# Exact first-layer outputs kept in their PSUM bank, and one ring of five banks, in an AdaLN block with a mixture of experts

## The chip, the cores and the metric

The kernel runs on one core of a Trainium2 chip. A core has five engines, each with its own in-order queue: TensorE (PE) for matmuls, VectorE (DVE) and ScalarE (ACT) for elementwise work, GpSimd (POOL) for elementwise work and indirect transfers, and SyncE (SP), which here only issues transfers. Matmul results land in PSUM, a memory of eight banks of 512 float32 columns by 128 partitions; everything else is in SBUF. The metric is the device time of one execution in microseconds (us). A smaller time is better.

## The reference

The reference is one transformer block on `x` of shape 2 x 2048 x 256: a layer norm with modulation, windowed attention with 16 heads, a residual add, a second layer norm with modulation, and a mixture of 8 experts of which each token uses 2. Only the expert part matters here. In short:

```python
logits = x @ gate_w.T + gate_b
probs = softmax(logits); topk_prob, topk_idx = top_k(probs, 2)
for c in range(2):
    # each token goes to a slot of its expert, up to 640 slots per expert and choice
    xb = slots of expert e
    hmid = relu(xb @ W1[e] + b1[e])        # 256 -> 1024
    yb = hmid @ W2[e] + b2[e]              # 1024 -> 256
    y = y + yb[slot of token] * prob
```

All of it is float32. The kernel keeps the precision by splitting every matmul operand into an upper part, rounded to a shorter float format, and a lower part, which is the exact value minus the upper one. A product is then three matmuls: upper with upper, upper with lower, lower with upper.

## The kernel before

The first 700 us or so are attention; the experts follow, and the first expert's first work is woven into the end of attention. The experts' work is cut into items: item `q` is an expert `e` with a range of row tiles of 128 slots (the list `items`). For experts 2 to 6 the first item has six tiles and is called wide here, and further items of two tiles, called short here, follow under an `If` on the number of filled slots (`further`, L1314 marks its branches). The items 0, 1 and 5 have two tiles and are placed by hand; from item 2 on a scheduler arranges the instructions of each stretch between two branches.

An item has eight steps `f`, one for each 128 of the 1024 hidden columns.
- `first_layer(q, f)` multiplies the turned slots `xT` with W1 into a PSUM bank `ph`. A wide item's 768 columns don't fit one bank, so it takes two chunks of 384 with a bank each. Six matmuls fill a chunk (L230, in `passes`). Then L1008 on ScalarE writes `hh`, the upper part of the relu, L1009 on VectorE computes the exact relu into an SBUF tile `r`, and L1010 on VectorE writes the lower part `hl = r - hh`. L1010 runs once for the whole step, over up to 768 columns. Both `hh` and `hl` carry the name `hm` in the profile.
- `second_layer(q, f)`, two steps later (`LAG`), multiplies `hm` with W2 and accumulates into `y`, three matmuls for each row tile.
- `scale_of` makes the tile `gw` of gates: L1044 on ScalarE and L1047 on VectorE, whose inputs `gbr` and `gw` both lie in SBUF. It runs in one step for each row tile of the item.
- `turn_slots` transposes the slots of a later item through a bank `tp_x` (L966) and splits them with L131 on ScalarE and L135 on VectorE.
- At the end of an item `results` adds the bias (L1063, VectorE, `ys<-y,b`), and `give` multiplies by the gates (L1073, GpSimd, `ys<-ys,gw`) and adds the rows to the output with indirect transfers (L1074, GpSimd). They run on GpSimd while TensorE is already in the next item.

PSUM during the experts: `ph` has three banks of its own, `y` three, and a ring of two serves everything else, the turned slots among it. `r` has one buffer, `hm` three for each part. In item 0 the ring of attention, six banks, serves all.

The lines of the scheduler's hints (`keep_in_program_order`) are not touched.

Of the kernel before, what the change touches and what calls it, by code (L numbers as in the profile page):

```python
# [8 lines left out]
FP = mybir.dt.float32  # L9
# [3 lines left out]
ALU = mybir.AluOpType  # L13
# [4 lines left out]
P = 128  # L18
# [10 lines left out]
def adaln_block_kernel(  # L29
# [18 lines left out]
    nc = tc.nc  # L48
# [4 lines left out]
    E, _, FF = w1.shape  # L53
# [35 lines left out]
    ring = {}  # L89

    def bank(name, shape=(P, 512)):
        return ring["pool"].tile(list(shape), FP, tag="ring", name=name, bufs=ring["bufs"])
# [132 lines left out]
    def passes(out_, pairs, start=True, stop=True, **kw):  # L225

        last = len(pairs) - 1
        for n, ((ah, al), (bh, bl)) in enumerate(pairs):
            for i, (a, b) in enumerate(((ah, bh), (ah, bl), (al, bh))):
                nc.tensor.matmul(  # L230
                    out=out_, lhsT=a, rhs=b,
                    start=start and n == 0 and i == 0,
                    stop=stop and n == last and i == 2, **kw,
                )
# [694 lines left out]
    def load_slots(q, more=0):  # L929

        e, tiles = items[q]
        hi = items[q + more][1].stop
        m = hi - tiles.start
        if q < 2:
            xt = (cl if q else early).tile([P, m, ROW], FP, tag="xt", name=f"xt_{q}", bufs=1)
        else:
            w = WIDE if m > 4 or not more else 4
            xt = mp.tile([P, w, ROW], FP, tag=f"xt{w}", name=f"xt_{q}", bufs=1 if w == 4 else 2)
        r0 = (E - e) * BUF - hi * P
        nc.sync.dma_start(  # L940
            out=xt[:, 0:m, :], in_=xbuf[r0 : r0 + m * P, :].rearrange("(n p) d -> p n d", p=P)
        )
        for i in range(q, q + more + 1):
            t = items[i][1]
            xts[i] = xt[:, hi - t.stop : hi - t.start, :]
# [28 lines left out]
    def first_layer(q, f):  # L974
        e, tiles = items[q]
        wa = experts[e].parts()[0]
        xh, xl = xTs[q]
        bias = b1T[:, e * NF + f : e * NF + f + 1]
        W = len(tiles) * P
        pool, w, bufs = (mp, WIDE * P, 1) if q else (early, W, 1)  # L980
        per = w // W
        if f % per == 0:
            first_layer.at = [
                pool.tile([P, w], FR, tag=f"hm{i}", name=f"hm{i}_{q}_{f}", bufs=2 + bufs)
                for i in range(2)
            ]
        o = (f % per) * W
        hh, hl = (a[:, o : o + W] for a in first_layer.at)
        r = pool.tile([P, w], FP, tag="r", name=f"r_{q}_{f}", bufs=1)
        nw = (W + 511) // 512  # L990
        for i in range(nw):
            s = slice(i * W // nw, (i + 1) * W // nw)
            if q:
                ph = pm_.tile([P, 512], FP, tag="ph", name=f"ph_{q}_{f}_{i}", bufs=3)
            else:
                ph = bank(f"ph_{q}_{f}_{i}")
            phv = ph[:, 0 : W // nw]
            passes(
                phv,
                [  # L1000
                    (
                        (wa[:, 0, d, f * P : (f + 1) * P], wa[:, 1, d, f * P : (f + 1) * P]),
                        (xh[:, d, s], xl[:, d, s]),
                    )
                    for d in range(ND)
                ],
            )
            nc.scalar.activation(hh[:, s], phv, AF.Relu, bias=bias)  # L1008
            nc.vector.tensor_scalar(r[:, s], phv, bias, 0.0, ALU.add, ALU.max)  # L1009
        nc.vector.tensor_tensor(hl, r[:, 0:W], hh, ALU.subtract)  # L1010
        hms[q, f] = (hh, hl)

    def second_layer(q, f, only=None):
# [107 lines left out]
    def layers(q):  # L1121

        for f in range(NF + LAG):
            if f < NF:
                first_layer(q, f)
            if f >= LAG:
                second_layer(q, f - LAG)
            n = f - 6 if q == 1 else f
            if q and 0 <= n < len(items[q][1]):
                scales[q, n] = scale_of(q, n)  # L1130
            yield
        for n0 in range(0, len(items[q][1]), 2):
            results(q, n0, 2)
# [111 lines left out]

    mp = ctx.enter_context(tc.tile_pool(name="moe", bufs=2, reuse_waits="tile"))
    pm_ = ctx.enter_context(tc.tile_pool(name="pmoe", bufs=1, space=PSUM, reuse_waits="tile"))
    ring.update(pool=pm_, bufs=2)
    load_slots(5)
    load_b2(1)  # L1250
    second = layers(1)
# [16 lines left out]
    def item(q, steps):  # L1268

        m = len(items[q][1])  # L1270
        for f in range(NF + (0 if narrow(q) else LAG)):
            if f < NF:
                first_layer(q, f)
            for step in steps.get(f, ()):
                step()
            if f >= LAG and not narrow(q):
                second_layer(q, f - LAG)
            n = f - 1 if q > 1 else f - 5
            if 0 <= n < m:
                scales[q, n] = scale_of(q, n)  # L1280
        if narrow(q):
            for n in range(m):
                for f in range(NF):
                    second_layer(q, f, n)
                results(q, n, 1)
                give()
        else:
            for n0 in range(0, m, 2):
                results(q, n0, min(2, m - n0))
            give()  # L1290
# [90 lines left out]
```

## Time and profile before

| | |
|---|---|
| median of three runs | 1149.95 us (1148.7 to 1150.23) |
| the profiled execution's own time | 1148.45 us |
| its span, first to last instruction | 1146.7 us |
| mean granted TensorE clock | 0.977 of full speed |
| TensorE busy | 1077.6 us, 94% |
| VectorE busy | 874.0 us, 76% |
| ScalarE busy | 678.0 us, 59% |
| GpSimd busy | 587.0 us, 51% |

In a profile line, `L1010 DVE TENSOR_TENSOR hm<-r,hm` is line 1010 of the kernel on VectorE, writing tile `hm` from tiles `r` and `hm`; shapes are partitions by columns; `xN` is a count. A timeline line starts with the start and the length in us and ends, in brackets, with the time its engine sat idle just before, and what ended that. `PEld` is TensorE's weight load. Matmuls are pipelined and their ends are modelled, so the distance from one matmul's start to the next one's is a better measure than the length of either: in a full stretch a matmul of 256 columns starts every 0.118 us, one of 384 every 0.166 us. The wide items lie at 843 to 878, 903 to 939, 953 to 989, 1014 to 1049 and 1074 to 1109 us.

### The profile page before, as it was taken

What the parts mean: (1) busy time and instruction counts of PE and PEld (TensorE: products, weight loads), DVE (VectorE), ACT (ScalarE), POOL (GpSimd) and SP (SyncE); (2) the same over time, 40 slices, a digit from 0 to 9 for tenths busy, and PEclk for the clock granted to TensorE, in tenths of its full rate; (3) what the DMA queues carried; (4) which work ended last, traced back from release to release, by engine and by line L of the source; (5) the groups of instructions that cost most, each with busy time, mean ns of one, the idle gap of its engine ahead of it and who ended that gap; (6) DMA issues with size and microseconds to landing.
All of it is one profiled execution on the core that took longest, in us unless ns stands there. A gap on an engine that the chain in (4) does not pass through costs nothing. (4 is left out here: it accounts for less than half of the span.)

```text
span 1146.7 us, 25186 instructions
## 1 busy us (share of the span) xinstructions
PE 1077.6 (94%) x9238; PEld 991.4 (86%) x9238; DVE 874.0 (76%) x2170; ACT 678.0 (59%) x2099; POOL 587.0 (51%) x767
## 2 busy tenths in 40 slices
PE   6799999999999999999999997788899999999995
PEld 4589999999999889999999996678799999999994
DVE  4667778878878778888888876677678787778773
ACT  3667677777777577777777776433444444344441
POOL 1345375575575555665665666444233525443524
PEclk9899999999999999999999998779999999999998
DMA  4866200000000010010010022233353434343413
GB/s 130 205 147 152 45 30 20 31 30 20 30 30 21 21 48 25 21 36 20 18 36 21 18 61 66 76 99 90 70 140 94 64 106 87 87 83 76 76 50 37
DMA packets 59863, 72.09 MB, mean 63 GB/s; under 512 B 4841, under 2 KB 51186, under 8 KB 59728
## 3 DMA queue, kind: packets, MB, share of 16 engines
q1 hardware_dynamic: 48016, 55.54, 17.1%
q0 software_dynamic: 11712, 14.79, 7.5%
q8 instruction: 80, 1.31, 0.5%
q14 instruction: 55, 0.45, 0.1%
HBM read 40.11 MB, written 32.27 MB: 63 GB/s over the span
## 5 line engine op out<-in xcount | busy, mean ns | idle before, releaser
L230 PE MATMUL pq<-hh,wq 128*128 128x256 f32 x1024 | 217.9, 297 | 7.8 <-DVE wq L135 5.4
L1008 ACT ACTIVATE hm<-ph,b1T 128x256 fp32r<-128x256 f32 (+2 forms) x184 | 99.2, 539 | 212.3 <-PE ph L230 182.3
L619 ACT ACTIVATE pm<-pm,mx 128x128 f32<-128x128 f32 x512 | 204.3, 403 | 15.7 <-DVE mx L605 15.6
L230 PE MATMUL y<-we,hm 128*128 128x256 f32 x1440 | 203.1, 285 | 6.2 <-DVE hm L1010 6.1
L230 PE MATMUL ph<-xT,we 128*128 128x256 f32 (+2 forms) x1104 | 199.2, 320 | 9.0 <-PEq L1314 3.6
L230 PEld LDWEIGHTS y<-we,hm 128*128 128x128 f32 x1440 | 186.9, 190 | 9.6 <-DVE hm L1010 8.3
L653 POOL TENSOR_SCALAR_AFFINE_SELECT pT<-pT 128x512 f32<-128x512 f32 (+1 forms) x128 | 79.8, 624 | 207.1 <-ACT pT L652 207.0
L230 PEld LDWEIGHTS ph<-xT,we 128*128 128x128 f32 x1104 | 168.2, 192 | 13.9 <-issue 4.2
L230 PEld LDWEIGHTS pq<-hh,wq 128*128 128x128 f32 x1024 | 170.8, 194 | 10.3 <-DVE wq L135 5.8
L230 PE MATMUL pq<-hl,wq 128*128 128x256 f32 x512 | 146.7, 287 | 0.6 <-DVE hl L278 0.6
L1009 DVE TENSOR_SCALAR r<-ph,b1T 128x256 f32<-128x256 f32 (+2 forms) x184 | 102.5, 563 | 58.6 <-ACT hm L1008 49.4
L629 POOL TENSOR_TENSOR pm<-pm,rd 128x512 f32<-128x512 f32 x128 | 133.6, 1044 | 26.0 <-DVE rd L627 26.0
L595 ACT COPY pm<-sc 128x256 f32<-128x256 f32 (+1 forms) x256 | 81.0, 362 | 107.0 <-PE sc L571 72.5
L1073 POOL TENSOR_TENSOR ys<-ys,gw 128x256 f32<-128x256 f32 x56 | 47.4, 942 | 171.3 <-DVE ys L1063 168.6
L676 PE MATMUL av<-pT,v 128*64 128x128 f32 (+1 forms) x1472 | 124.5, 317 | 5.2 <-ACT v L326 1.8
L676 PEld LDWEIGHTS av<-pT,v 128*64 128x64 f32 x1472 | 89.7, 138 | 33.2 <-issue 3.5
L596 DVE COPY_PREDICATED pm<-within,sc 128x256 f32<-128x256 int32 (+1 forms) x256 | 96.1, 422 | 24.9 <-ACT pm L595 23.8
L1074 POOL DMA_INDIRECT out_dram<-ys,tok x60 | 97.2, 1620 | 28.0 <-issue 12.1
L571 PE MATMUL sc<-kr,qh 64*128 64x256 f32 (+1 forms) x1024 | 102.5, 294 | 1.4 <-DVE ql L308 1.2
L230 PEld LDWEIGHTS pq<-hl,wq 128*128 128x128 f32 x512 | 99.6, 195 | 0.9 <-DVE hl L278 0.9
L619 ACT ACTIVATION_READ_ACCUMULATOR pm<-pm,mx 128x1 f32 x512 | 99.8, 195 | 0.0
L1010 DVE TENSOR_TENSOR hm<-r,hm 128x256 fp32r<-128x256 f32 (+2 forms) x144 | 95.2, 661 | 5.4
(166 smaller groups left out, 2249.5 us busy)
## 6 DMA issues: line engine op xcount, KB each, us to landing
raw_w<-in_L_ffn_W_dram SPq DMA_DIRECT2D x32, 512.0 KB, 3.7
xbuf<-blank SPq DMA_DIRECT2D x16, 685.0 KB, 10.1
xt<-xbuf SPq DMA_DIRECT2D x7, 822.0 KB, 6.5
xt<-xbuf SPq DMA_DIRECT2D x8, 548.0 KB, 4.9
x<-in_L_attn_x_dram SPq DMA_DIRECT2D x16, 256.0 KB, 2.9
out_dram<-x SPq DMA_DIRECT2D x16, 256.0 KB, 2.2
raw_wq<-in_L_attn_Wqkv_dram SPq DMA_DIRECT2D x6, 512.0 KB, 4.1
wm<-in_L_wmod_dram SPq DMA_DIRECT2D x3, 512.0 KB, 5.3
```

The costliest lines, as they stand in the source:

```text
L230: nc.tensor.matmul(out=out_, lhsT=a, rhs=b, start=start and n == 0 and i == 0, stop=stop and n == last and i == 2, **kw,)
L571: nc.tensor.matmul(out=sc[h][:, t, lo:], lhsT=q[r, t * P : (t + 1) * P], rhs=kr[r, (0, 1, 0)[i], hp, blk, :], start=(i == 0), stop=(i == 2),)
L595: nc.scalar.copy(pm[:, h, ts, :], blocks[:, own, :])
L596: nc.vector.copy_predicated(pm[:, h, ts, :], within.rearrange("p (a k) -> p a k", a=1).to_broadcast([P, n, P]), blocks[:, before, :],)
L619: nc.scalar.activation(pm[:, h, t, :], pm[:, h, t, :], AF.Exp, bias=mx[:, h, t : t + 1], accum_out=den[:, h, t : t + 1],)
L629: nc.gpsimd.tensor_tensor(pmv, pmv, rd.rearrange("p h (t a) -> p (h t) a", a=1).to_broadcast([P, 2 * SBT, P]), ALU.mult,)
L653: nc.gpsimd.affine_select(out=pT[:, :, t0:, 0, :], in_=own[:, :, t0:, :], pattern=[[0, 2], [0, n], [-1, P]], compare_op=ALU.is_gt, fill=0. ...
L676: nc.tensor.matmul(out=av[h * DH : (h + 1) * DH, q0 : q0 + hi - lo], lhsT=v[:, f0 + h * DH : f0 + (h + 1) * DH], rhs=pT[:, h, lo:hi], star ...
L1008: nc.scalar.activation(hh[:, s], phv, AF.Relu, bias=bias)
L1009: nc.vector.tensor_scalar(r[:, s], phv, bias, 0.0, ALU.add, ALU.max)
L1010: nc.vector.tensor_tensor(hl, r[:, 0:W], hh, ALU.subtract)
L1074: add = nc.gpsimd.indirect_dma_start(out=of, out_offset=bass.IndirectOffsetOnAxis(ap=tok[:, 0:1], axis=0), in_=y, in_offset=None, bounds_c ...
```

## The change

In `first_layer`, the exact relu is no longer written to an SBUF tile `r`. VectorE writes it in place, over the matmul's output in the PSUM bank, and the subtraction takes it from there. The subtraction moves into the loop over the chunks: a wide step has two of 384 columns instead of one of 768. The tile `r` is gone. The bank of a chunk is in use until its subtraction is done, where it was free after the relu. And `ph` has no banks of its own any more: with the turned slots and the other small users it shares a ring of five banks, where there were three and two. The number of `y` banks is as before.

```diff
         hh, hl = (a[:, o : o + W] for a in first_layer.at)
-        r = pool.tile([P, w], FP, tag="r", name=f"r_{q}_{f}", bufs=1)
         nw = (W + 511) // 512
         for i in range(nw):
             s = slice(i * W // nw, (i + 1) * W // nw)
-            if q:
-                ph = pm_.tile([P, 512], FP, tag="ph", name=f"ph_{q}_{f}_{i}", bufs=3)
-            else:
-                ph = bank(f"ph_{q}_{f}_{i}")
+            ph = bank(f"ph_{q}_{f}_{i}")
             phv = ph[:, 0 : W // nw]
             passes(
...
             nc.scalar.activation(hh[:, s], phv, AF.Relu, bias=bias)
-            nc.vector.tensor_scalar(r[:, s], phv, bias, 0.0, ALU.add, ALU.max)
-        nc.vector.tensor_tensor(hl, r[:, 0:W], hh, ALU.subtract)
+            nc.vector.tensor_scalar(phv, phv, bias, 0.0, ALU.add, ALU.max)
+            nc.vector.tensor_tensor(hl[:, s], phv, hh[:, s], ALU.subtract)
         hms[q, f] = (hh, hl)
...
-    ring.update(pool=pm_, bufs=2)
+    ring.update(pool=pm_, bufs=5)
```

With four lines fewer, the relu is L1005 and the subtraction L1006 in the changed kernel, the ScalarE relu L1004, the gates L1040 and L1043, the bias L1059 and the multiplication by the gates L1069.

## Prediction

> **What bounds the kernel now.** I read the totals of the page first, then the busy times by stage, then TensorE's waits in the second half of the span, and last the timeline around the waits that touch the changed lines.
>
> Busy time, share of the span and instructions of each engine:
>
> ```profile
> PE 1077.6 (94%) x9238; PEld 991.4 (86%) x9238; DVE 874.0 (76%) x2170; ACT 678.0 (59%) x2099; POOL 587.0 (51%) x767
> ```
>
> The two VectorE groups that the change touches, shapes kept apart (busy us, mean ns of one, idle before):
>
> ```profile
> L1009 DVE TENSOR_SCALAR r<-ph,b1T 128x384 f32<-128x384 f32 x80 | 48.1, 615 | 29.2 <-ACT hm L1008 26.5 <-DVE hm L1010 0.5
> L1010 DVE TENSOR_TENSOR hm<-r,hm 128x256 fp32r<-128x256 f32 x88 | 46.0, 522 | 2.6
> L1010 DVE TENSOR_TENSOR hm<-r,hm 128x768 fp32r<-128x768 f32 x40 | 38.2, 956 | 2.2
> ```
>
> TensorE is the bound. By stage (columns: length, then busy time of PE, PEld, DVE, ACT, POOL), one wide item of six row tiles, then a short item of two with the exit behind it:
>
> ```profile
> 903.00:939.00 36.00, 35.99 (x261) 35.75 (x261) 27.40 (x42) 16.99 (x30) 6.37 (x10) 1.00 0.41 110
> 939.00:953.00 14.00, 12.26 (x104) 11.86 (x102) 11.88 (x23) 4.99 (x11) 12.45 (x11) 1.00 0.36 40
> ```
>
> A wide item leaves TensorE no gap, and VectorE 8.6 us of 36. Only the short items have gaps. TensorE's waits from 700 us on (total, times, longest):
>
> ```profile
> PE tp_x L966 <- DMA xt<-xbuf: 7.8, 2, 5.6
> PE y L230 <- DVE hm L1010: 6.1, 9, 0.9
> PE ph L230 <- DVEq L1314: 2.9, 3, 1.1
> ```
>
> No wait of `ph` on a bank is in this list: three banks for `ph` already suffice. The change can only reach the second line. Timeline of one such wait, in the first short item after a wide one:
>
> ```profile
> 942.28 1.69 POOL L1074 DMA_INDIRECT out_dram<-ys,tok  x1 [0.15 <-POOL ys L1073]
> 943.35 0.47 DVE L1047 SCALAR_TENSOR_TENSOR gw<-gbr,xt,gw 128x256 f32<-128x256 f32 x1
> 943.42 1.99 POOL L1073 TENSOR_TENSOR ys<-ys,gw 128x256 f32<-128x256 f32 x2
> 943.74 1.97 DVE L1010 TENSOR_TENSOR hm<-r,hm 128x256 fp32r<-128x256 f32 x1
> 944.47 0.39 PE L230 MATMUL y<-we,hm 128*128 128x256 f32 x2
> 945.76 0.74 PE L230 MATMUL y<-we,hm 128*128 128x256 f32 x4 [0.90 <-DVE hm L1010]
> ```
>
> A subtraction that takes 0.42 us elsewhere takes 1.97, as long as GpSimd's pair of multiplications lasts. Two matmuls need 0.24 us and the next begins 1.29 later: 1.05 us lost. The same happens at 885.11, 995.20 and 1055.72. In the second short item the victim is L1047 instead:
>
> ```profile
> 893.75 2.01 POOL L1073 TENSOR_TENSOR ys<-ys,gw 128x256 f32<-128x256 f32 x2
> 894.63 1.43 DVE L1047 SCALAR_TENSOR_TENSOR gw<-gbr,xt,gw 128x256 f32<-128x256 f32 x1
> 896.45 0.98 PE L230 MATMUL y<-we,hm 128*128 128x256 f32 x6 [0.41 <-DVE hm L1010]
> ```
>
> That loses 0.55 to 0.57 us, three times (896.45, 1006.48, 1067.00). Together 4.2 + 1.7 = 5.9 us. Of the nine waits the other two, at 783.62 and 787.28, stand behind the routing chain in VectorE's queue.
>
> **What the Trainium skill says.** "SBUF — State Buffer", section "Who interferes with whom": a VectorE instruction with two SBUF inputs contends with a GpSimd instruction that reads SBUF, one with at most one does not. The trace agrees. Minimum, median and maximum in ns:
>
> ```profile
> L1010 DVE TENSOR_TENSOR hm<-r,hm x144: 411/457/1971, 730.5 to 1131.0; 128x256 fp32r<-128x256 f32 x88, 128x768 fp32r<-128x768 f32 x40, 128x512 fp32r<-128x512 f32 x16
> L1047 DVE SCALAR_TENSOR_TENSOR gw<-gbr,xt,gw x60: 473/476/1441, 764.8 to 1121.9; 128x256 f32<-128x256 f32 x60
> L308 DVE TENSOR_TENSOR al<-av,ah x128: 411/416/425, 55.9 to 753.0; 128x256 fp32r<-128x256 f32 x128
> L135 DVE TENSOR_TENSOR xT<-tp_x,xT x35: 659/681/692, 720.6 to 1130.4; 128x512 fp32r<-128x512 f32 x35
> ```
>
> L308 and L135 take one input from PSUM and never stretch. "PSUM — Partial Sum Buffer", section "PSUM bank collisions raise a hardware error": two engines must be kept apart by bank. That order exists already (L1009 waits for ACT L1008 49.4 us, 47 times), so in-place writing adds no wait between engines. On an in-place VectorE operation in PSUM I found no price, and no row of this trace has VectorE writing PSUM.
>
> **The change part by part.**
>
> *Subtraction from PSUM.* It loses one of its two SBUF inputs. Price of one: 416 ns at 256 columns (L308), 681 at 512 (L135), so about 550 at 384. In short items 416 against 420: nothing. In a wide item 16 x 0.55 replace 8 x 0.956: +1.15 us VectorE, and 8 more dependent pairs cost some 0.1 us each (a dependent instruction starts 0.51 after the 0.48 us one, an independent one 0.40): +2 us. Cover: the 8.6 us VectorE leaves free there. Without cover it would be 5 x 2 = 10 us. First halves of `hm` come earlier, which TensorE doesn't need: it has lag 2.
>
> *`r` goes.* With its single buffer, each L1009 waited for the L1010 before it: in the short item 941.07 to 941.63, 0.56 against the 0.34 of independent neighbours. So 0.2 us go per step, two steps before the stretched subtraction.
>
> *In-place write.* Bounds for one L1009: gain 0.06 (the writing side shorter) to double streaming (from 482 at 256 and 749 at 512, 1.04 ns per column: +0.4 us at 384). I take no difference[...].
>
> *Five shared banks.* A bank is now free one subtraction later (0.42 to 0.55 us), but comes round after five uses; at two first-layer chunks (2 us) and second-layer work of 2.1 us per wide step that is 8 us or more, against 1 + 0.6 + 0.6 + 0.6 us from first matmul to release. Hidden. The early item in the attention part keeps its six-bank ring; its half microsecond more is hidden likewise.
>
> *Order.* From item 2 on a scheduler arranges the instructions. The changed program issues four or five `ph` before the first `y` of a short item (three before), and both chunks of a wide step together. In the second short item this puts the `y` of step 1 at 44 matmuls (5.2 us) instead of 38 (4.5) after the start, and its `hm` is ready at 5.0 even in the old timing: the 0.57 us gap closes. GpSimd's and SP's queues are unchanged in order.
>
> *Where the stall of the first short item goes.* The subtraction no longer waits, so ask what does: the next VectorE instruction with two SBUF inputs beside GpSimd's pair is the second L1047. Times from the item's first `ph` (939.08): now L1047 starts at +4.27 and GpSimd's pair at +4.34, so L1047 just escapes. After: VectorE is 0.4 earlier, L1047 at +3.87. But the last step of the wide item now ends its first output pair 12 matmuls before the end instead of 8 (0.47 us), GpSimd starts that much earlier, and loses the 0.18 us for which its fourth multiplication waited for L1010 (0.92 us, against 0.74 of the others): pair at +3.69. L1047 is then 0.18 too late, waits for the pair's end (+5.6), the subtraction behind it ends at +6.4, and TensorE, which wants it at +5.55, loses 0.9 instead of 1.05.
>
> **Sum, likeliest case.** Second short items 3 x 0.57 = 1.7; first ones 4 x 0.15 = 0.6; routing stretch and other small queue savings 0.4: 2.7 us. Span 1146.7 - 2.7 = 1144.0. The profiled execution took 1148.45 (1.75 around its span), 1.5 below the median 1149.95, and I carry the difference to that median: **1147.2 us**.
>
> **Rivals.**
> - *The stall vanishes* (30%): the pair and L1047 swap, since 0.18 us decides and three in-place writes of 0.06 less would do it. For it: L1047 escapes by 0.07 today. Against: the arithmetic above. All four places act alike: 4.2 + 1.7 + 0.5 = 6.4, so 1143.5.
> - *Nothing moves* (16%): closed gaps reopen a few matmuls later, because the short item has 11.3 us of matmuls and its last subtraction follows its last `ph` by 1.62 us, against 14 matmuls (1.65 us) of cover. About 1149.5.
> - *In-place writing streams at half speed* (12%): +0.4 us x 16 = 6.4, with the 2 above 8.4 us per wide item, on 27.4 busy and about 4 us of unavoidable idling at its ends: 39.8 for 36. Five items: +19 us, some +16 net, 1166. It decides from about +0.16 us per 384-column L1009. For it: reading and writing one bank; against: no trace either way.
>
> **How the numbers follow.** Likeliest case 42%, own range 1145.8 to 1148.8. The range takes in it, the vanished stall and nothing moving, leaving out the slow write and tails: 1142.8 to 1150.8. 0.2% of 1149.95 is 2.3 us, about what a measurement can tell. Faster: 30% + 60% of 42% + little = 56%. Same: the rest of 42% and most of 16% = 29%. Slower: 12% + tails = 15%.
>
> **What would show it.** Right: the subtraction at most 0.43 us at 256 columns and 0.57 at 384 everywhere; L1047 stretched to some 2 us four times; TensorE waiting about 0.75 us in four first short items, not at all in the second ones; L1005 (was L1009) still 0.48 and 0.62. Wrong: no stretched L1047 (first rival); L1005 over 0.78 at 384 with TensorE gaps in wide items (last rival); `ph` waiting for the subtraction, meaning banks do bind.

## The result, and the profile after

The changed kernel takes 1141.91 us (median of four runs, 1140.21 to 1142.62) where the kernel before took 1150.09 in the same comparison (four runs, 1148.7 to 1150.56): ratio 0.9929, 95% interval 0.9911 to 0.9946. A second comparison, further below, gave 0.9938 (0.9926 to 0.9950). The prediction was 1147.2 with a range from 1142.8 to 1150.8. Direction right, size wrong: 8.2 us came where 2.8 were forecast, and the time lies 0.9 us below the range.

The profiled execution has a span of 1140.1 us, 6.6 less than before. Busy time of the engines on the page of the changed kernel:

```profile
PE 1075.5 (94%) x9238; PEld 991.1 (87%) x9238; DVE 868.0 (76%) x2210; ACT 680.5 (60%) x2099; POOL 581.3 (51%) x767
```

TensorE's work is the same 9238 matmuls. Its busy time fell by 2.1 us and its idle time by 4.5; as the ends of matmuls are modelled, busy time takes in some waiting. The relu in place (384 columns) and the subtraction (384 and 256), shapes kept apart (busy us, mean ns of one, idle before):

```profile
L1005 DVE TENSOR_SCALAR ph<-ph,b1T 128x384 f32<-128x384 f32 x80 | 49.3, 620 | 17.0 <-ACT hm L1004 15.9
L1006 DVE TENSOR_TENSOR hm<-ph,hm 128x384 fp32r<-128x384 f32 x80 | 43.9, 555 | 4.2
L1006 DVE TENSOR_TENSOR hm<-ph,hm 128x256 fp32r<-128x256 f32 x88 | 36.6, 420 | 2.2
```

Writing in place costs 620 ns at 384 columns where the relu into SBUF cost 615: next to nothing. The subtraction, 420 ns at 256 columns, is at the price of the rows that read PSUM (416). Minimum, median and maximum, in ns, of the subtraction and of the gate scaling:

```profile
L1006 DVE TENSOR_TENSOR hm<-ph,hm x184: 406/546/692, 730.7 to 1124.5; 128x256 fp32r<-128x256 f32 x88, 128x384 fp32r<-128x384 f32 x80, 128x512 fp32r<-128x512 f32 x16
L1043 DVE SCALAR_TENSOR_TENSOR gw<-gbr,xt,gw x60: 471/476/1460, 764.6 to 1115.6; 128x256 f32<-128x256 f32 x60
```

The subtraction is never stretched: its maximum is that of 512 columns, where before one of 256 took up to 1971. The gate scaling still is, up to 1.46 us. TensorE's waits from 700 us on (total, times, longest):

```profile
PE tp_x L966 <- DMA xt<-xbuf: 7.0, 3, 5.4
...
PE ph L230 <- DVEq L1310: 2.9, 3, 1.1
...
PE y L230 <- DVE hm L1006: 1.2, 2, 0.9
```

Of nine waits for `hm` two are left, the pair behind the routing chain near 784 us. No wait of `ph` on a bank has come. The seven waits in the short items are gone, the first ones too, which the prediction had kept. Timeline of a first short item of the changed kernel (it starts at 985.84), one view for each engine, GpSimd, VectorE and then TensorE:

```profile
989.44 2.29 POOL L1069 TENSOR_TENSOR ys<-ys,gw 128x256 f32<-128x256 f32 x2
```

```profile
989.30 0.48 DVE L1005 TENSOR_SCALAR ph<-ph,b1T 128x256 f32<-128x256 f32 x1
989.69 1.46 DVE L1043 SCALAR_TENSOR_TENSOR gw<-gbr,xt,gw 128x256 f32<-128x256 f32 x1
991.07 0.41 DVE L1006 TENSOR_TENSOR hm<-ph,hm 128x256 fp32r<-128x256 f32 x1
```

```profile
991.24 0.40 PE L230 MATMUL y<-we,hm 128*128 128x256 f32 x2
991.48 0.40 PE L230 MATMUL ph<-xT,we 128*128 128x256 f32 x2
991.72 0.63 PE L230 MATMUL y<-we,hm 128*128 128x256 f32 x4
992.18 0.63 PE L230 MATMUL ph<-xT,we 128*128 128x256 f32 x4
```

GpSimd's pair comes at +3.60, the second gate scaling at +3.85, and it is stretched, as forecast. But it ends at +5.31, while the pair runs on to +5.89, and the subtraction behind it ends at +5.64. The matmuls start 0.24, 0.24 and 0.46 us apart, for two, two and four: no loss.

**Where the time went.** From here on I use one measure, the tail, which leaves out the changing start of the expert part: from the first matmul of the wide item at 842.8 us (the "ninth item" of the expectations) to the end of the span. Before it is 1146.7 - 842.83 = 303.9 us, after 1140.1 - 842.84 = 297.3: the whole 6.6 us lies here. A first short item takes 11.94 us (878.39 to 890.33) for 13.00, a second one 11.47 (890.33 to 901.80) for 12.27. The other first ones gained 0.93, 1.15 and 0.99, the other second ones 0.88 and 0.73, so the seven short items make 6.5 of the 6.6. The wide items are equal (35.55 and 35.59). The median fell by 1.6 us more than that in the first comparison, by 0.4 more in the second: the interval of either ratio takes in 6.6 us (0.9943).

### The profile page after: what moved, and what is told of

It reads as the page before. It is cut to its first block, busy times and chain, and to the rows that moved or that the text cites. A ratio compares the mean times of both kernels' runs of the same rounds, so it can differ in the third digit from the quotient of the medians.

```text
span 1140.1 us, 25126 instructions
## 1 busy us (share of the span) xinstructions
PE 1075.5 (94%) x9238; PEld 991.1 (87%) x9238; DVE 868.0 (76%) x2210; ACT 680.5 (60%) x2099; POOL 581.3 (51%) x767
## 5 line engine op out<-in xcount | busy, mean ns | idle before, releaser
L1004 ACT ACTIVATE hm<-ph,b1T 128x256 fp32r<-128x256 f32 (+2 forms) x184 | 99.1, 539 | 206.3 <-PE ph L230 112.3
L230 PE MATMUL ph<-xT,we 128*128 128x256 f32 (+2 forms) x1104 | 192.4, 320 | 8.5 <-PEq L1310 3.3
L230 PE MATMUL y<-we,hm 128*128 128x256 f32 x1440 | 195.0, 284 | 1.3 <-DVE hm L1006 1.2
L230 PEld LDWEIGHTS y<-we,hm 128*128 128x128 f32 x1440 | 181.1, 190 | 2.9 <-DVE hm L1006 1.6
L1005 DVE TENSOR_SCALAR ph<-ph,b1T 128x256 f32<-128x256 f32 (+2 forms) x184 | 103.8, 567 | 50.6 <-ACT hm L1004 47.6
L1069 POOL TENSOR_TENSOR ys<-ys,gw 128x256 f32<-128x256 f32 x56 | 46.8, 939 | 171.1 <-DVE ys L1059 168.4
L1070 POOL DMA_INDIRECT out_dram<-ys,tok x60 | 94.9, 1582 | 28.2 <-issue 11.1
L230 PE MATMUL po<-wo,ah 128*128 128x256 f32 x512 | 98.6, 286 | 0.0
```

Of the source, the lines that this page charges most:

```text
L230: nc.tensor.matmul(out=out_, lhsT=a, rhs=b, start=start and n == 0 and i == 0, stop=stop and n == last and i == 2, **kw,)
L1005: nc.vector.tensor_scalar(phv, phv, bias, 0.0, ALU.add, ALU.max)
L1069: (nc.vector if items[q][0] == E - 1 else nc.gpsimd).tensor_tensor(y, y, gw_, ALU.mult)
L1070: add = nc.gpsimd.indirect_dma_start(out=of, out_offset=bass.IndirectOffsetOnAxis(ap=tok[:, 0:1], axis=0), in_=y, in_offset=None, bounds_c ...
```

## The experiments

"A" in the expectations is my theory: the gain is the subtraction's escape from GpSimd's multiplications, as it has only one input in SBUF. The main rival, "B", is that the ring of five banks, which lets TensorE's order run ahead, does it alone. All ten runs stand in one table. The tail is the measure above; "first" and "second" are the lengths of the first and second short item near 880 us, and "no gates" leaves out GpSimd's multiplication of the results by their gates from item 2 on, the last expert's apart.

| kernel | median, us | ratio (95%) | tail, us | first | second |
|---|---|---|---|---|---|
| before (its profile) | | | 303.9 | 13.00 | 12.27 |
| before, PSUM only | 1144.85 | 0.9969 (0.9957 to 0.9981) | 300.2 | 12.16 | 11.98 |
| before, ring only | 1149.38 | 1.0009 (1.0002 to 1.0015) | 304.0 | 12.95 | 12.10 |
| before, `r` twice | 1146.36 | 0.9983 (0.9976 to 0.9990) | 303.4 | 12.80 | 12.36 |
| before, ring and `r` twice | 1142.63 | 0.9952 (0.9939 to 0.9964) | 301.4 | 12.80 | 11.49 |
| before, no gates | 1141.23 | 0.9943 (0.9930 to 0.9956) | 296.5 | 11.76 | 11.43 |
| after (its profile; timed again) | 1141.93 | 0.9938 (0.9926 to 0.9950) | 297.3 | 11.94 | 11.47 |
| after, no gates | 1139.13 | 0.9921 (0.9908 to 0.9934) | 297.7 | 11.77 | 11.49 |
| after, one multiply | 1142.74 | 0.9943 (0.9930 to 0.9956) | 297.8 | 11.93 | 11.70 |
| after, last pair one | 1140.13 | 0.9924 (0.9905 to 0.9943) | 298.3 | 12.07 | 11.47 |
| after, relu twice | 1141.75 | 0.9937 (0.9916 to 0.9957) | 297.9 | 12.07 | 11.47 |

The kernel before had medians of 1148.36, 1148.89 and 1148.38 beside these. Tail and median don't always agree. The tail and the item lengths come from one profiled execution of each kernel. The part ahead of the tail ranges from 838.8 to 844.5 us over the profiles; the last section explains part of that.

### The operand in PSUM alone

```diff
-        r = pool.tile([P, w], FP, tag="r", name=f"r_{q}_{f}", bufs=1)
...
-            nc.vector.tensor_scalar(r[:, s], phv, bias, 0.0, ALU.add, ALU.max)
-        nc.vector.tensor_tensor(hl, r[:, 0:W], hh, ALU.subtract)
+            nc.vector.tensor_scalar(phv, phv, bias, 0.0, ALU.add, ALU.max)
+            nc.vector.tensor_tensor(hl[:, s], phv, hh[:, s], ALU.subtract)
```

> The kernel before with the exact output kept in PSUM and subtracted chunk by chunk, but the old banks (three for the first layer, two for turned slots). Theory A (the subtraction no longer shares SBUF with GpSimd): the four waits of about 1 us in first short items go, the three of 0.57 us in second short items stay, because the stretched gate scaling is unchanged and the order of the matmuls there is the old one: 4.2 us less, about 1146, subtraction at most 0.43 us at 256 columns. Theory B (the ring of five lets TensorE run ahead, and that is the gain): 1150, waits as before. Theory C (writing in place is dear): above 1155.

Measured: 3.5 us less by the medians, 3.7 in the tail. Subtraction and gate scaling in this kernel, and the waits of TensorE's weight loads from 842 us on:

```profile
L1009 DVE TENSOR_TENSOR hm<-ph,hm x184: 406/545/693, 729.3 to 1125.4; 128x256 fp32r<-128x256 f32 x88, 128x384 fp32r<-128x384 f32 x80, 128x512 fp32r<-128x512 f32 x16
L1046 DVE SCALAR_TENSOR_TENSOR gw<-gbr,xt,gw x60: 473/476/1308, 763.1 to 1116.4; 128x256 f32<-128x256 f32 x60
PEld ph L230 <- DVEq L1313: 2.3, 2, 1.3
PEld y L230 <- DVE hm L1009: 1.8, 10, 0.2
```

Theory A's size, nearly: the first short items are 0.76 to 0.83 us shorter, 3.1 us in all. A's other half did not come as forecast: the three waits of 0.57 us did not stay, and the second short items are 0.21 to 0.30 us shorter. The gate scaling is held for long in the second short items only. In a first one (984.89) it comes at +3.85 and GpSimd's pair at +4.12, and it takes 0.60 us, hardly more than its usual 0.47; in the changed kernel the pair is at +3.59. What the prediction said of the pair, that the new order brings it about half a microsecond earlier, is thus seen from both sides. What remains are ten small waits, 0.2 us each, for a subtraction that comes just behind its matmul: in this kernel 18 first-layer matmuls go ahead of an item's first `y`, as before; in the changed kernel 24 in a first short item and 28 in a second. This edit also takes away `r`; a freed `r` alone is tested further below.

### The ring of five alone

```diff
-            if q:
-                ph = pm_.tile([P, 512], FP, tag="ph", name=f"ph_{q}_{f}_{i}", bufs=3)
-            else:
-                ph = bank(f"ph_{q}_{f}_{i}")
+            ph = bank(f"ph_{q}_{f}_{i}")
...
-    ring.update(pool=pm_, bufs=2)
+    ring.update(pool=pm_, bufs=5)
```

> The kernel before with the ring of five alone; the exact output still goes to SBUF and is subtracted for the whole step. Theory A: the subtraction is still stretched to 1.97 us in first short items and TensorE still loses about 1 us there, four times; only the three waits of 0.57 us go: 1.7 us less, about 1148.4. Theory B: nearly the whole gain, 1142 to 1143, no waits.

Measured: no gain, by the median 1.0 us slower (0.2 to 1.7). Rival B falls. The subtraction is stretched as before, and in a first short item two matmuls still take 1.30 us where they need 0.24. TensorE's timeline in the first short item, then in the second:

```profile
995.65 0.40 PE L230 MATMUL y<-we,hm 128*128 128x256 f32 x2
996.95 0.74 PE L230 MATMUL y<-we,hm 128*128 128x256 f32 x4 [0.90 <-DVE hm L1007]
...
1011.88 3.66 PE L230 MATMUL y<-we,hm 128*128 128x256 f32 x22
1015.38 0.85 PE L230 MATMUL ph<-xT,we 128*128 128x384 f32 x4
```

Theory A's 1.7 us from the second short items did not come either. Their 0.57 us gap has gone from its place, and reopened at the item's end: the last 22 matmuls take 3.50 us, 0.90 more than 22 x 0.118 = 2.60; before, they took 2.81 there. VectorE's rows at that end say why:

```profile
1012.75 0.48 DVE L1006 TENSOR_SCALAR r<-ph,b1T 128x256 f32<-128x256 f32 x1
1013.27 0.42 DVE L1007 TENSOR_TENSOR hm<-r,hm 128x256 fp32r<-128x256 f32 x1
1013.80 0.48 DVE L1006 TENSOR_SCALAR r<-ph,b1T 128x256 f32<-128x256 f32 x1
```

With one buffer `r`, relu and subtraction are a chain of 1.05 us a step, each waiting for the other. VectorE, once late, can't catch up. This is the rival "nothing moves" of the prediction, real, but only where `r` stays.

### Two buffers for `r`, without and with the ring

```diff
-        r = pool.tile([P, w], FP, tag="r", name=f"r_{q}_{f}", bufs=1)
+        r = pool.tile([P, w], FP, tag="r", name=f"r_{q}_{f}", bufs=2 if q else 1)
```

> The kernel before with two buffers for the exact output in SBUF instead of one; everything else as before. Theory A (the stall is a meeting in time of GpSimd's pair and an instruction with two SBUF inputs, and the one buffer's wait of 0.2 us a step makes VectorE late): the subtraction comes 0.2 to 0.4 us earlier, and either escapes the pair by under 0.1 us (4 us less, about 1146), or is still caught (1150). Theory D (the buffer's wait is the whole cost): 6 us less, about 1144, with no stretched instruction anywhere.

Measured: 2.0 us less by the median, but 0.5 in the tail, and the first short items only 0.1 to 0.2 shorter. The subtraction comes earlier and is still caught, 2.04 us long. A's second branch, then, so far as the tail goes. Where the other 1.5 us of the median lie isn't shown: the profiled execution took 1148.47 us, 2.1 above this kernel's median.

> The kernel before with the ring of five and two buffers for the exact output in SBUF: both freedoms that the change gives beside the operand in PSUM. Theory A (the operand in PSUM is needed): the subtraction is still stretched to 2 us and TensorE loses 1 us in each of four first short items; at most the gap of 0.6 us in second short items goes: 1146.5 to 1148.5. Rival (slack is enough, the operand is not needed): 1142 to 1143.

The median is the rival's number: 1142.63, nearly the changed kernel's and outside theory A's 1146.5 to 1148.5. The trace says where it comes from. The tail is 2.5 us shorter, not 6.6; the other 4.0 us lie ahead of it, where the changed kernel gained nothing (838.8 us in place of 842.8). The subtraction of this kernel; VectorE and GpSimd in the first short item that starts at 983.56; and TensorE's wait there:

```profile
L1007 DVE TENSOR_TENSOR hm<-r,hm x144: 407/470/2045, 729.5 to 1124.5; 128x256 fp32r<-128x256 f32 x88, 128x768 fp32r<-128x768 f32 x40, 128x512 fp32r<-128x512 f32 x16
```

```profile
987.55 0.60 DVE L1044 SCALAR_TENSOR_TENSOR gw<-gbr,xt,gw 128x256 f32<-128x256 f32 x1
988.07 2.03 DVE L1007 TENSOR_TENSOR hm<-r,hm 128x256 fp32r<-128x256 f32 x1
```

```profile
987.81 1.99 POOL L1070 TENSOR_TENSOR ys<-ys,gw 128x256 f32<-128x256 f32 x2
```

```profile
988.96 0.40 PE L230 MATMUL y<-we,hm 128*128 128x256 f32 x2
990.15 0.63 PE L230 MATMUL y<-we,hm 128*128 128x256 f32 x3 [0.80 <-DVE hm L1007]
```

Two matmuls take 1.19 us: the stall of the first short item is there, 0.95 of its 1.05 us. The second short items are whole, 11.49 us as in the changed kernel. So the ring and a freed `r` together close the second short items, which neither alone does, and take 2.7 us from the seven short items; the first ones need the operand in PSUM, which alone took 3.9. The two make the changed kernel's 6.5. The 4.0 us ahead of the tail stay open: 1.4 of them is the clock behind the branch (last section), 1.5 a shorter idle time at that branch (2.15 for 3.65 us). Whether this edit brings them or chance does, one profile can't say; by the metric this kernel is within 0.7 us of the changed one.

### Without GpSimd's multiplication

```diff
-            (nc.vector if items[q][0] == E - 1 else nc.gpsimd).tensor_tensor(y, y, gw_, ALU.mult)
+            if q < 2 or items[q][0] == E - 1:
+                (nc.vector if items[q][0] == E - 1 else nc.gpsimd).tensor_tensor(y, y, gw_, ALU.mult)
```

> The kernel before with GpSimd's multiplication of the results by the gates left out from item 2 on (the last expert keeps its own, on VectorE). Theory A: no subtraction and no gate scaling is stretched, all seven waits go: 5.9 us less, about 1144. Theory B: GpSimd is not what costs: 1150. If the changed kernel's 8 us are all contention: 1142.

Measured: 7.1 us less by the medians, 7.4 in the tail, and no wait of `y` for `hm` after 842 us. Without the multiplications, the kernel before is at least as fast as the changed one, with its old banks and its old `r`. GpSimd's multiplications are what all seven waits came from.

> The changed kernel with GpSimd's multiplication by the gates left out from item 2 on (the last expert keeps its own, on VectorE). Theory A: the gate scalings that are still stretched (1.3 to 1.45 us, seven of them) cost TensorE nothing, so leaving out what stretches them gives nothing: within 1 us of the changed kernel. Rival: a rest of the contention is still paid, 1 to 2 us less.

In the changed kernel leaving them out gives nothing in the tail: 297.7 against 297.3. The seven short items are 0.1 us shorter in all, so the gate scalings, stretched to 1.3 to 1.46 us in seven places, cost TensorE next to nothing; the first wide item is 0.6 us longer (36.11 for 35.55), with a gap at its start. The median is 2.8 us lower; in the profiled execution, the stretch behind the branch at 814 us is 3.0 us shorter (last section).

### How long the second gate scaling is shut out

The changed kernel again, to have its own spread:

> The changed kernel itself, timed again in more runs. If the gain is the closed waits and nothing else, as the two profiled spans say (6.6 us), the ratio is near 0.9943, about 1141.9 beside 1148.4. If something that the spans do not show adds 1.6 us, as the first comparison of four runs against four had it, 0.9929. TensorE waits for the subtraction twice, near 784 us, and nowhere after.

Measured 0.9938, between the two, both inside its interval; the tail of its profile is 297.3 again. The 6.6 us are the change's; no run shows that it gives more.

The prediction had the gate scaling wait for the end of both multiplications. It waited 0.97 us (1.44 less 0.47, its usual length). To see whether it is let in between the two, they were made one. First everywhere, by laying the gates of two row tiles side by side in one tile (the lines that build it are left out here):

```diff
...
-            (nc.vector if items[q][0] == E - 1 else nc.gpsimd).tensor_tensor(y, y, gw_, ALU.mult)
+            if q < 2 or narrow(q):
+                (nc.vector if items[q][0] == E - 1 else nc.gpsimd).tensor_tensor(y, y, gw_, ALU.mult)
+            elif n % 2 == 0:
+                ys, gg = whole.pop((q, n)), gws.pop((q, n // 2))
+                (nc.vector if items[q][0] == E - 1 else nc.gpsimd).tensor_tensor(ys, ys, gg, ALU.mult)
```

> The changed kernel, with the gates of two row tiles side by side in one tile, so that GpSimd multiplies a pair of results in one instruction of 512 columns instead of two of 256. Theory A (what failed in the prediction is the length of the wait: the second gate scaling was let in after one of the two multiplications): now it waits for the whole, its length is 1.8 us or more in first short items, the subtraction behind it ends at about +6.4 us after the item's start, and TensorE loses 0.7 to 0.9 us four times: 3 us more, about 1145. Theory E (TensorE's order now gives cover enough, whatever the wait): as the changed kernel, 1142.

This run didn't test it. The order on GpSimd changed: its three multiplications ran in one go (985.67 to 989.45), ahead of the scatter, and were done before the second gate scaling came (990.39). The first one was held 0.43 us instead. Tail 297.8. In second short items the scaling took up to 1.78 us, and the item 0.23 us longer. So only the last pair of a wide item was joined, the four before left as they are:

```diff
...
-            (nc.vector if items[q][0] == E - 1 else nc.gpsimd).tensor_tensor(y, y, gw_, ALU.mult)
+            if q < 2 or n < 4:
+                (nc.vector if items[q][0] == E - 1 else nc.gpsimd).tensor_tensor(y, y, gw_, ALU.mult)
+            elif n == 4:
+                nc.gpsimd.tensor_tensor(whole[q], whole[q], gws[q], ALU.mult)
```

> The changed kernel, where of a wide item's six results only the last two are multiplied by their gates in one instruction of 512 columns; the four before stay single, with the scatter between as before. So GpSimd is busy at the same place in the first short item as in the changed kernel (+3.6 us), but with one instruction. Theory A (the second gate scaling was let in between the two multiplications): it now waits for the end of the one, its length in first short items grows from 1.45 to 1.8 us or more, the subtraction behind it ends at +6.0 to +6.4, and TensorE loses 0.4 to 0.8 us in each of four places: 1.6 to 3.2 us more from the ninth item to the end (297.3 in the changed kernel). Theory F (the wait has a length of its own, near 1 us, whatever GpSimd's instructions are): 1.45 us as before, no loss.

Timeline of the first short item that starts at 984.23, GpSimd, VectorE and TensorE:

```profile
987.81 1.87 POOL L1079 TENSOR_TENSOR ys<-ys,gw 128x512 f32<-128x512 f32 x1
988.08 1.90 DVE L1048 SCALAR_TENSOR_TENSOR gw<-gbr,xt,gw 128x256 f32<-128x256 f32 x1
989.90 0.41 DVE L1006 TENSOR_TENSOR hm<-ph,hm 128x256 fp32r<-128x256 f32 x1
```

The multiplication is at +3.58, the scaling at +3.85: the meeting of the changed kernel to 0.02 us. Now the scaling takes 1.90 us, in all four first short items (1.89 to 1.90). That is 0.45 more than beside two instructions, as theory A had it, and against a fixed wait of 1 us. The subtraction ends at +6.08, and two matmuls from 989.63 take 0.74 us: 0.50 lost. The deadline of this item is therefore near +5.58, and the prediction's +5.55 fits it. It is not the deadline of all four: beside the changed kernel this item is 0.63 us longer, two others 0.13 and 0.12, and the fourth (1043.60) is as long, though its subtraction ends at +6.08 too. The scheduler had put more first-layer matmuls there between. The loss in the tail is 1.0 us in all, less than the 1.6 expected at least. The median, lower than the changed kernel's, says nothing on 1 us.

The last experiment made the subtraction late in another way:

```diff
             nc.vector.tensor_scalar(phv, phv, bias, 0.0, ALU.add, ALU.max)
+            if q > 1 and f == 2 and len(tiles) == 2 and len(items[q - 1][1]) == 6:
+                nc.vector.tensor_scalar(phv, phv, 0.0, 0.0, ALU.add, ALU.max)
```

> The changed kernel, where in the short item after each wide one the third step's bias and relu is done twice in place (the second changes nothing): 0.5 us more on VectorE right before or behind the second gate scaling, so the third subtraction ends at about +6.1 us instead of +5.6. Theory A (the deadline of the prediction, +5.55, was right, only the wait was shorter): TensorE loses 0.4 to 0.5 us there, five times at most: 1.6 to 2.5 us more from the ninth item to the end. Theory E (the new order gives cover enough): no loss, under 0.5 us in all.

Some 0.4 us more on VectorE cost 0.7 us in the tail over all four places that ran (of the five in the program). The subtraction ended at +6.34 (991.91, item from 985.57), yet TensorE lost little there: the item took 11.94 us, in the changed kernel 11.78. The scheduler had moved the `y` matmuls back behind more of `ph`. So this run says nothing on the old deadline. It says that the order is fitted to the program, and that with five banks it had room here for most of that delay.

## Why the prediction was wrong, point by point

- **Step "first short items", the failed one.** The prediction said: "L1047 is then 0.18 too late, waits for the pair's end (+5.6), the subtraction behind it ends at +6.4, and TensorE, which wants it at +5.55, loses 0.9 instead of 1.05." The meeting came as forecast: pair at +3.59 (forecast +3.69), scaling at +3.84 (+3.87), stretched in four places. The length was wrong: 1.45 us, not some 2.2. I took the stall of the subtraction before (1.97 us) for the price of meeting the pair. That subtraction had waited through both multiplications, until 0.13 us before the pair's end; the scaling was let in with 1.05 us of the pair to come. So the subtraction ended at +5.63 in the item at 878.39, where six matmuls lost 0.14 us, and at +5.64 in the item at 985.84, where none was lost. In the item at 937.30 the scheduler had put the next relu ahead of it; it ended at +6.01, and none was lost either. So the deadline of +5.55 was not one for all four items. A loss of four times 0.9 was forecast and nearly none came: that is some 3.5 us of the miss.
- **Why the wait was shorter.** The form of the instruction isn't it: in the second short items the same scaling was kept out to 0.18 us before the pair's end. Nor is the time of arrival: in the kernel with ring and `r` twice the subtraction came 0.26 us behind the pair's start, as the scaling did in the changed kernel (0.25), and waited through both. The nine profiles with a pair of separate multiplications have 55 meetings from 870 us on in which a VectorE instruction of 256 columns took over 0.6 us and overlapped both, and they fall in two groups. In 39, VectorE was in an instruction with two SBUF inputs when the pair began (the gate scaling at 987.55 above), and the one that waited got in 0.13 to 0.18 us before the pair's end. In 16, VectorE was then in one that reads PSUM, or just starting it (the relu in place at 989.30 above), and the one that waited got in with 1.05 us left. There is no exception, but no run changes this alone, so it is a pattern, and the cause stays open. In the changed kernel the pair comes earlier, into a relu in place, and the prediction had counted on the other case.
- **The vanished stall.** Its number, 1143.5, was nearer, its reason wrong: pair and scaling did not swap. They meet, and the meeting is cheap enough.
- **Second short items, and the order.** Right that four or five first-layer chunks start ahead of an item's first `y` (24 and 28 matmuls, 18 before) and that the gap closes. It gave 0.73 to 0.88 us each, not 0.57: the 0.2 us at the item's end went too. The 0.4 us that the sum has for the routing stretch and small queue savings did not come: the part ahead of the tail is 842.84 us for 842.83.
- **The `r` step.** Counted at 0.2 us a step, nothing on its own. Right alone (0.5 us in the tail), but undervalued: the ring without it gains nothing, since the gap moves to the item's end. That is the rival "nothing moves", seen where `r` stays.
- **In-place write, price of the subtraction, five banks.** Right: 620 for 615 ns, 420 for 416, 555 for 550, VectorE 1.2 us busier in a wide item (28.61 for 27.43 us; 1.15 were forecast for the work, 2 with the waits) and covered, no wait for a bank.
- **The time.** 1.4 us of the miss is not in the kernel: I started from 1149.95 of three runs, where the later medians of before are 1148.4 to 1148.9.

The Trainium skill, "SBUF — State Buffer", section "SBUF: two separate sides", says that of a VectorE instruction with two SBUF inputs and a GpSimd one that reads SBUF, the one that starts first blocks the other for the whole instruction. The run of the joined pair agrees: one instruction of twice the columns held the scaling 1.43 us (1.90 less 0.47) for 0.97. Which side goes next when GpSimd has a second instruction waiting, the page doesn't say, and here both were seen.

## What to carry to other kernels

The stall that one instruction suffers isn't the price for the next one that meets the same resource: here 1.55 us of waiting became 0.97. Ask through how many of the other engine's instructions it will wait, and how much slack its reader has. Slack that a scheduler can use (more banks) and a chain that is cut (a single buffer gone) may each be worth nearly nothing and 2.5 us together, so test them together as well as apart. With differences of a few microseconds compare a stretch of the trace that begins behind the variable part; by its median alone, the kernel with ring and `r` twice would here have passed for the whole explanation.

## What the runs showed of the hardware that was not expected

- **The clock behind a branch.** At about 814 us TensorE idles 2 to 4 us at a branch. What follows runs at half clock for a while in some profiles and at full clock in others, with the same work. The length of the idle time doesn't decide: it was 3.35 us in the changed kernel and 3.37 in the changed kernel without gates. The traces show what does. All changes of the granted clock in a profile lie multiples of 3.41 us apart, on a grid whose place differs from profile to profile. By stretches of that grid (length, busy PE, PEld, DVE, ACT, POOL, granted clock), first the changed kernel, then the one without gates (its grid is that of its changes at 771.62 and 1126.61 us):

```profile
810.37:813.78 3.41, 0.81 (x7) 0.61 (x6) 0.75 (x2) 0.00 (x0) 1.62 (x3) 1.00 0.02 5
813.78:817.19 3.41, 2.66 (x6) 2.15 (x7) 0.00 (x0) 0.00 (x0) 3.10 (x3) 0.50 0.39 91
817.19:820.61 3.42, 3.42 (x9) 2.64 (x8) 1.45 (x2) 1.22 (x2) 0.19 (x1) 0.50 0.80 210
```

```profile
809.17:812.58 3.41, 1.59 (x14) 1.39 (x12) 1.45 (x3) 0.11 (x1) 0.33 (x1) 1.00 0.03 7
812.58:815.99 3.41, 1.86 (x8) 1.59 (x9) 0.00 (x0) 0.15 (x1) 2.97 (x3) 1.00 0.29 30
815.99:819.41 3.42, 3.42 (x16) 2.80 (x16) 2.74 (x5) 2.49 (x5) 0.18 (x1) 1.00 0.93 263
```

  In the first, 2.60 us of the idle time fall into one stretch, and the next runs at half clock; it has 0.75 us idle itself, so the half clock lasts for another, and ends after one without idle. In the second the idle time is split into 1.82 and 1.55 us, and the clock stays full. At this branch, over the twelve profiles, a stretch at full clock with 2.1 us idle or more was followed by half clock, one with 1.6 or less was not, and near 1.8 both were seen; elsewhere in the traces both are seen from 1.3 to 2.3. So the half clock lasts 0, 3.41 or 6.83 us, and from the branch to the wide item it takes 25.3 to 25.5 us (without gates; ring and `r` twice), 26.9 to 27.0 (before and its other variants) or 27.8 to 28.4. The Trainium skill, "TensorE: Matmul & The Clock Gate", section "Part 1: The HAM clock gate", says that the clock halves after an idle window of about 3.4 us, and that the windows run freely. The grid agrees; but here a window was enough that was idle for 2.1 us of it. This stretch accounts for up to 3 us of what the profiles differ by ahead of the tail. Where it starts differs too, from 812.6 to 817.5 us, and that is not explained.
- **Writing a PSUM bank in place** with VectorE costs almost what writing to SBUF does: 485 ns for 482 at 256 columns, 620 for 615 at 384.
- **Two GpSimd multiplications that meet a stretched scaling** in a first short item took 2.29 us together where they take 1.43 alone and took 1.99 beside the old subtraction; GpSimd had slack for it.
